# The last tile of a sparse attention kernel as 128 rows instead of 127, with the spare row dropped at the scatter

## The chip, the cores and the metric

The kernel runs on one core of one Trainium2 chip. The metric is the device time of one execution in microseconds (us), from three runs of the kernel before. The profile is of one more execution. A core has five engines that work side by side and wait for one another through semaphores: TensorE (PE, its weight loads shown as PEld), VectorE (DVE), ScalarE (ACT), GpSimd (POOL) and SyncE (SP). Transfers between the chip's main memory and the on-chip memory are done by 16 DMA engines.

## The reference, cut to what matters

```python
def reference(x, adj, Wf, bf, Wg, bg, W, bW):            # x: 3327 x 1024, adj: 3327 x 3327, 0 or 1
    h = jnp.maximum(_layernorm(x, axis=-1), 0.0)
    f = h @ Wf + bf
    g = h @ Wg + bg
    e = jax.nn.relu(f @ g.T)
    scores = jnp.where(adj > 0, e, -9e15)
    attention = jax.nn.softmax(scores, axis=1)
    return x + attention @ (h @ W + bW)
```

The graph is sparse: a node has itself and some 16 neighbours on average, so of each row of 3327 scores only a few count.

## The kernel before, in words

The rows (nodes) are handled in tiles of P = 128. There are 3327 = 25 x 128 + 127 nodes, so NT = 26 tiles, and the last one (number 25) has 127 rows; `rows(t)` gives the count.

**First part** (to about 300 us). For each tile of nodes in their given order the kernel normalises x into `hd` (main memory, one row of 1024 numbers, 4 KB, per node), reads the adjacency rows, and makes a list of up to KM = 40 neighbour numbers with the node's degree behind them, stored in `pd` (41 numbers per node). Beside that, TensorE makes A = Wf Wg^T. At its end the nodes are sorted by falling degree: `perm[p, s]` (line 594) is the number of the node that stands at place p of tile s. A place that no node is sorted to holds 0, which in this kernel is place 127 of tile 25. After the sort `make_rows()` (line 595) makes a few bias rows on PE and VectorE. Where the direct transfers of this part would have 127 rows, `pieces(t)` cuts them in two, 112 rows and 15.

**Second part** (the rest). It goes over the 26 tiles of sorted nodes. `CAPS[s]` is the largest degree that tile s may have: 37 for tile 0, then falling to 14, 13, 13, 12, 11 for tiles 21 to 25. If any node were over its cap, `bads` (line 655) would be set and a slow dense path would follow; with these inputs it does not run. For tile s:

- `prepare(s)`: GpSimd gathers the lists `pi` and the rows `hp` of the tile's own nodes by `perm` (indirect DMA, one row per partition, helper `gather`, line 621). PE transposes `hp` and multiplies it by A into `q` (lines 632, 650, 651), ScalarE copies `q` out (652).
- `dot(s, k)` for k below the cap: GpSimd gathers `G`, the rows of `hd` of everybody's k-th neighbour (line 621); VectorE multiplies it with `q` and sums along the row into one score per node (line 668, output `junk`).
- `softmax` over the scores (lines 678 to 694).
- `combine`: y = sum of score times `G`. VectorE does one step per k (line 734), ScalarE the first (732); in tiles with a cap over 13 some of the steps go through ScalarE and PE (728, 711).
- `project(s)`: GpSimd gathers the rows `xp` of x; PE transposes y (711), ScalarE copies it (744), PE multiplies with W into `ps_o` (749, 750).
- `finish(s)`: VectorE adds `ps_o` to `xp` (758), and GpSimd scatters `xp` to the output rows by `perm` (indirect DMA, line 759).

In program order `prepare(s + 2)` stands behind `project(s)`, the dots of the next chunk stand 3 ahead (`AHEAD`), and `finish(s - 1)` stands behind the dots of tile s. The framework's scheduler then sets the final order per engine. `G` has 23 buffers, so gather number i waits until gather number i - 23 has been read for the last time; `pi` has 3 buffers, `q`, `hp`, `xp` and y two. All indirect DMAs are issued by GpSimd, one after the other, and a wait at the head of its queue holds back every gather behind it.

In the last tile every one of these operations takes the partitions `[:n]` with n = 127: one gather of `pi`, one of `hp`, 11 of `G`, one of `xp` and the scatter.

Of the kernel before, what the change touches and what calls it, by code (L numbers as in the profile page):

```python
# [8 lines left out]
FP = mybir.dt.float32  # L9
I32 = mybir.dt.int32  # L10
AF = mybir.ActivationFunctionType
# [10 lines left out]
KM = 40  # L22
# [266 lines left out]
def edge_path(ctx: ExitStack, tc: tile.TileContext, x, adj, Wf, bf, Wg, bg, W, bW, out, flag):  # L289
# [23 lines left out]
    def rows(t):  # L313
        return min(P, N - t * P)
# [25 lines left out]

    perm = const.tile([P, NT], I32, name="perm")
    A_sb = wts.tile([P, KD, QW], FP, name="A_sb")
# [23 lines left out]
    with ExitStack() as part1:  # L366
# [227 lines left out]
        nc.vector.scalar_tensor_tensor(perm, ps[:, :NT], float(P), tens, op0=ALU.mult, op1=ALU.add)  # L594
        make_rows()
# [32 lines left out]
    def transposed2(to, of, n):  # L628
        for g in range(0, KD, 4):
            ps = p_t.tile([P, 4, P], FP, name="ps_t")  # L630
            for k in range(4):
                nc.tensor.transpose(ps[:, k, :n], of[:n, (g + k) * P : (g + k + 1) * P], ident[:n, :n])
            nc.scalar.copy(to[:, g : g + 4, :n], ps[:, :, :n])  # L633
# [3 lines left out]
    def prepare(s):  # L637
        n = rows(s)
        e = st[s] = {"n": n}
# [5 lines left out]
        transposed2(hT, hp, n)  # L645
        q = e["q"] = qpool.tile([P, QW], FP, name="q")
        for o in range(0, QW, QB):
            ps = p_q.tile([P, CB], FP, name="ps_q")
            for k in range(KD):
                nc.tensor.matmul(ps[:n, :QB], hT[:, k, :n], A_sb[:, k, o : o + QB], start=(k == 0), stop=False)  # L650
            nc.tensor.matmul(ps[:n, :QB], ones3[:, :n], v3[:, o : o + QB], start=False, stop=True)
            nc.scalar.copy(q[:n, o : o + QB], ps[:n, :QB])  # L652
        df = small.tile([P, 1], FP, name="df")
        nc.vector.tensor_copy(df[:n], pi[:n, KM : KM + 1])
        nc.vector.tensor_scalar(bads[:n, s : s + 1], df[:n], float(CAPS[s]), None, op0=ALU.is_gt)
        mask = e["mask"] = small.tile([P, KM], FP, name="mask")
        nc.vector.tensor_scalar(mask[:n], iotak[:n], df[:n], NEG, op0=ALU.is_ge, op1=ALU.mult)
        e["sc"] = small.tile([P, KM], FP, name="sc")
# [3 lines left out]
    def dot(s, k):  # L662
        e = st[s]
        n = e["n"]
# [3 lines left out]
        nc.vector.tensor_tensor_reduce(  # L668
            junk[:n], g[:n], e["q"][:n, :D], 1.0, e["q"][:n, D : D + 1], op0=ALU.mult, op1=ALU.add,
            accum_out=e["sc"][:n, k : k + 1],  # L670
        )

    def softmax(s, k0, k1, last):

        e = st[s]
        n = e["n"]
        sc = e["sc"][:n, k0:k1]
        nc.vector.scalar_tensor_tensor(sc, sc, 0.0, e["mask"][:n, k0:k1], op0=ALU.max, op1=ALU.add)
        nm = small.tile([P, 1], FP, name="nm")
        nc.vector.tensor_reduce(nm[:n], sc, AX.X, ALU.max, negate=True)  # L680
        if k0:
            nc.vector.tensor_tensor(nm[:n], nm[:n], e["nm"][:n], op=ALU.min)
        l = small.tile([P, 1], FP, name="l")
        nc.scalar.activation(sc, sc, AF.Exp, bias=nm[:n], accum_out=l[:n])
        if k0:
            al = small.tile([P, 1], FP, name="al")
            nc.scalar.activation(al[:n], e["nm"][:n], AF.Exp, bias=nm[:n], scale=-1.0)
            nc.vector.scalar_tensor_tensor(l[:n], e["l"][:n], al[:n], l[:n], op0=ALU.mult, op1=ALU.add)
        if last:
            rs = small.tile([P, 1], FP, name="rs")  # L690
            nc.vector.reciprocal(rs[:n], l[:n])
            if k0:
                nc.vector.tensor_tensor(al[:n], al[:n], rs[:n], op=ALU.mult)
            nc.vector.tensor_scalar(sc, sc, rs[:n], None, op0=ALU.mult)
        if k0:
            nc.scalar.activation(e["y"][:n], e["y"][:n], AF.Copy, scale=al[:n])
        e["nm"], e["l"] = nm, l
# [7 lines left out]
    def sum_transposed(e, g, first, last):  # L705

        n = e["n"]
        if first:
            e["yT"] = p_y.tile([P, KD, P], FP, name="yT_ps")
        for c in range(KD):  # L710
            nc.tensor.matmul(  # L711
                e["yT"][:, c, :n], g[:n, c * P : (c + 1) * P], ident[:n, :n], is_transpose=True,
                start=(first and c % 4 == 0), stop=(last and c % 4 == 3), skip_group_check=True,
            )

    def combine(s, k0, k1, last):
        e = st[s]
        n = e["n"]
        if not k0:
            e["y"] = ypool.tile([P, D], FP, name="y")  # L720
        y = e["y"][:n]
        e["first"] = True
        pe = on_tensor(s, k0, k1) if last else []
        for k in range(k0, k1):
            p = e["sc"][:n, k : k + 1]
            g = G[s, k]
            if k in pe:
                nc.scalar.activation(g[:n], g[:n], AF.Copy, scale=p)  # L728
                sum_transposed(e, g, e["first"], False)
                e["first"] = False  # L730
            elif k == 0:
                nc.scalar.activation(y, g[:n], AF.Copy, scale=p)  # L732
            else:
                nc.vector.scalar_tensor_tensor(y, g[:n], p, y, op0=ALU.mult, op1=ALU.add)  # L734

    def project(s):
        e = st[s]
        n = e["n"]
        e["xp"] = xpool.tile([P, D], FP, name="xp")
        gather(e["xp"][:n], x[:, :], perm[:n, s : s + 1])  # L740
        yT = yTpool.tile([P, KD, P], FP, name="yT")
        sum_transposed(e, e["y"], e["first"], True)
        for g in range(0, KD, 4):
            nc.scalar.copy(yT[:, g : g + 4, :n], e["yT"][:, g : g + 4, :n])  # L744
        e["o"] = []
        for o in range(OH):
            ps = p_o.tile([P, CB], FP, name="ps_o")
            for k in range(KD):
                nc.tensor.matmul(ps[:n], yT[:, k, :n], W_sb[:, k, o * CB : (o + 1) * CB], start=(k == 0), stop=False)  # L749
            nc.tensor.matmul(ps[:n], ones3[:, :n], bW3[:, o * CB : (o + 1) * CB], start=False, stop=True)  # L750
            e["o"].append(ps)

    def finish(s):
        e = st[s]
        n = e["n"]
        for o in range(OH):
            xo = e["xp"][:n, o * CB : (o + 1) * CB]
            nc.vector.tensor_add(xo, e["o"][o][:n], xo)  # L758
# [91 lines left out]
```

## Time and profile before

| | us |
|---|---|
| median of the three runs (lowest, highest) | 1500.97 (1500.28, 1507.38) |
| profiled execution, its own time | 1504.68 |
| span of the profiled execution, first to last instruction | 1502.9 |
| VectorE busy | 1274.7 (85%) |
| PE busy | 1165.0 (78%) |
| GpSimd busy | 891.9 (59%) |
| ScalarE busy | 442.9 (29%) |

A row of the groups gives the line, engine and operation, output <- input by the program's names, then "xcount | busy us, mean ns of one | idle time of the engine just before them, and what ended it". In the rows in order of time the first number is the start in us from the span's start, the second the length in us; in square brackets stands the idle time of that engine before it and what ended it. In the answers on DMA the digits are tenths of the 16 engines' time in 40 equal slices of the window that was asked for, and under them stand the GB/s that were moved in each slice; "us to landing" runs from the issue of a transfer to its last byte.

### The profile page before, as it was taken

Reading aid. Unit: us, or ns where it says so; the run is one execution under the profiler, and the core shown is the slowest. Engines: PE = TensorE matmul, PEld = TensorE weight load, DVE = VectorE, ACT = ScalarE, POOL = GpSimd, SP = SyncE. Lnnn points to the kernel's source line nnn. Section 1 sums busy time; section 2 is a strip of 40 time slices with the busy share of each in tenths; the row PEclk is TensorE's granted clock in tenths of the full one; section 3 lists DMA queues with packets and bytes.
Section 4 is the critical chain, followed back from the end, with each engine's and each line's share of the span. In section 5 each row is a group of like instructions: output and inputs, shape, how many; then the busy total and the mean of one; then the engine's idle time right before and its main releaser. Section 6 shows DMA issues by size and latency. Waiting matters only on the chain.

```text
span 1502.9 us, 13875 instructions
## 1 busy us (share of the span) xinstructions
PE 1165.0 (78%) x4242; PEld 660.4 (44%) x4242; DVE 1274.7 (85%) x2645; ACT 442.9 (29%) x673; POOL 891.9 (59%) x627
## 2 busy tenths in 40 slices
PE   1259899284298989999898889999999899695262
PEld 1125453052165545555554455555554455342030
DVE  5878887959979999999888899999999999696360
ACT  6656676111144223342222212223121211110000
POOL 7677767346567667646655565667576666374310
PEclk9999899687698999999998989999999999897676
DMA  9797887268687898868766777788787777384310
GB/s 339 286 357 272 321 282 259 82 233 324 205 308 277 292 323 309 297 225 322 265 206 233 263 281 281 280 293 282 252 276 257 253 255 232 126 321 101 86 44 16
DMA packets 124445, 372.57 MB, mean 248 GB/s; under 512 B 41025, under 2 KB 41425, under 8 KB 121033
## 3 DMA queue, kind: packets, MB, share of 16 engines
q0 software_dynamic: 106288, 286.92, 55.6%
q1 hardware_dynamic: 10860, 70.49, 12.9%
q10 hardware_dynamic: 7212, 14.18, 2.5%
q8 instruction: 35, 0.57, 0.2%
q14 instruction: 50, 0.41, 0.1%
HBM read 343.63 MB, written 27.80 MB: 247 GB/s over the span
## 4 chain that ended last, share of the span: by engine, by line
DVE 28%; PE 24%; issue 20%; POOL 12%; DMA 11%; ACT 3%; POOLq 0%; ACTq 0%; DVEq 0%
DVE y L734 12%; PE ps_o L749 12%; DMA G<-hd,pi 9%; DVE junk L668 6%; POOL r L446 5%; POOL G L621 5%; PE ps_q L650 5%; PE yT_ps L711 4%; DVE cand L455 3%; PE ps_A L522 2%; DMA pi<-pd,perm 1%; PE ps_A L540 1%; DVE xp L758 1%; ACT r L445 1%; DVE sc L668 1%
## 5 line engine op out<-in xcount | busy, mean ns | idle before, releaser
L621 POOL DMA_INDIRECT G<-hd,pi x468 | 572.6, 1223 | 307.2 <-ACT y L732 95.5
L668 DVE CUSTOM_DVE_ANT_0 junk<-G,q 128x1024 bf16<-128x1024 f32 (+1 forms) x468 | 601.1, 1284 | 80.7 <-DMA G<-hd,pi 78.1
L650 PE MATMUL ps_q<-A_sb,hT 128*128 128x342 f32 (+1 forms) x1248 | 395.1, 466 | 74.8 <-ACT q L652 64.8
L734 DVE SCALAR_TENSOR_TENSOR y<-G,sc,y 128x1024 f32<-128x1024 f32 (+1 forms) x320 | 411.3, 1285 | 4.8 <-ACT y L732 2.8
L749 PE MATMUL ps_o<-W_sb,yT 128*128 128x512 f32 (+1 forms) x832 | 388.0, 621 | 9.9 <-ACT yT L744 9.7
L650 PEld LDWEIGHTS ps_q<-A_sb,hT 128*128 128x128 f32 (+1 forms) x1248 | 232.8, 194 | 195.4 <-ACT q L652 67.1
L749 PEld LDWEIGHTS ps_o<-W_sb,yT 128*128 128x128 f32 (+1 forms) x832 | 161.2, 199 | 208.7 <-issue 190.0
L446 POOL TENSOR_TENSOR r<-r,iotaj 128x3327 f32<-128x3327 f32 (+1 forms) x26 | 187.8, 7227 | 74.6 <-ACT r L445 59.8
L455 DVE MAX8 cand<-r 128x8 f32<-128x208 f32 (+2 forms) x416 | 134.3, 362 | 34.8 <-POOL r L446 34.8
L652 ACT COPY q<-ps_q 128x342 f32<-128x342 f32 (+1 forms) x78 | 32.7, 449 | 342.3 <-DVE sc L668 249.2
L728 ACT ACTIVATE G<-G,sc 128x1024 f32<-128x1024 f32 x122 | 129.0, 1137 | 0.0
L522 PE MATMUL ps_A<-WgT,WfT 128*128 128x512 f32 x256 | 122.4, 638 | 2.9 <-ACT WfT L496 2.9
L711 PE MATMUL yT_ps<-ident,G 128*128 128x128 f32 x976 | 116.8, 277 | 2.1 <-ACT G L728 2.1
L711 PEld LDWEIGHTS yT_ps<-ident,G 128*128 128x128 f32 x976 | 108.5, 142 | 12.6 <-ACT G L728 5.5
L633 ACT COPY hT<-ps_t 128x512 f32<-128x512 f32 (+1 forms) x52 | 30.1, 593 | 192.2 <-PE ps_q L650 159.9
L711 PE MATMUL yT_ps<-ident,y 128*128 128x128 f32 (+1 forms) x208 | 34.4, 320 | 67.4 <-DVE y L734 49.8
L744 ACT COPY yT<-yT_ps 128x512 f32<-128x512 f32 (+1 forms) x52 | 27.8, 586 | 198.2 <-PE yT_ps L711 198.0
L522 PEld LDWEIGHTS ps_A<-WgT,WfT 128*128 128x128 f32 x256 | 51.4, 205 | 75.9 <-issue 66.0
L759 POOL DMA_INDIRECT out_dram<-xp,perm x26 | 35.0, 1346 | 77.6 <-DVE xp L758 71.8
L445 ACT ACTIVATE r<-a 128x3327 f32<-128x3327 int32 (+1 forms) x26 | 77.1, 2967 | 8.7 <-issue 4.8
L758 DVE TENSOR_TENSOR xp<-ps_o,xp 128x512 f32<-128x512 f32 (+1 forms) x52 | 35.7, 686 | 34.5 <-PE ps_o L750 34.4
L711 PEld LDWEIGHTS yT_ps<-ident,y 128*128 128x128 f32 (+1 forms) x208 | 28.7, 166 | 72.5 <-DVE y L734 37.3
(134 smaller groups left out, 760.0 us busy)
## 6 DMA issues: line engine op xcount, KB each, us to landing
a<-in_adj_dram SPq DMA_DIRECT2D x25, 1663.5 KB, 9.0
xt<-in_x_dram SPq DMA_DIRECT2D x25, 512.0 KB, 4.9
hd<-xt ACTq DMA_DIRECT2D x25, 512.0 KB, 5.4
G<-hd,pi POOLq DMA_INDIRECT x468, 6.3
wr<-in_L_gnn_Wg_dram SPq DMA_DIRECT2D x8, 512.0 KB, 6.5
wr<-in_L_gnn_Wf_dram SPq DMA_DIRECT2D x8, 512.0 KB, 5.7
W_sb<-in_L_gnn_W_dram SPq DMA_DIRECT2D x1, 4096.0 KB, 16.5
a<-in_adj_dram SPq DMA_DIRECT2D x1, 1455.6 KB, 11.1
```

Of the source, the lines that this page charges most:

```text
L445: nc.scalar.activation(r[:n], a[:n], AF.Relu, accum_out=deg[:n, t : t + 1])
L446: nc.gpsimd.tensor_mul(r[:n], r[:n], iotaj[:n])
L455: nc.vector.max(cand[:n, s * 8 : s * 8 + 8], r[:n, s * SW : min(N, (s + 1) * SW)])
L522: nc.tensor.matmul(ps, WfT[:, k, :], WgT[:, k, o * CB : (o + 1) * CB], start=(k == 0), stop=(k == KD - 1))
L621: nc.gpsimd.indirect_dma_start(out=to, out_offset=None, in_=table, in_offset=bass.IndirectOffsetOnAxis(ap=idx, axis=0),)
L650: nc.tensor.matmul(ps[:n, :QB], hT[:, k, :n], A_sb[:, k, o : o + QB], start=(k == 0), stop=False)
L668: nc.vector.tensor_tensor_reduce(junk[:n], g[:n], e["q"][:n, :D], 1.0, e["q"][:n, D : D + 1], op0=ALU.mult, op1=ALU.add, accum_out=e["sc"] ...
L711: nc.tensor.matmul(e["yT"][:, c, :n], g[:n, c * P : (c + 1) * P], ident[:n, :n], is_transpose=True, start=(first and c % 4 == 0), stop=(la ...
L728: nc.scalar.activation(g[:n], g[:n], AF.Copy, scale=p)
L734: nc.vector.scalar_tensor_tensor(y, g[:n], p, y, op0=ALU.mult, op1=ALU.add)
L749: nc.tensor.matmul(ps[:n], yT[:, k, :n], W_sb[:, k, o * CB : (o + 1) * CB], start=(k == 0), stop=False)
L758: nc.vector.tensor_add(xo, e["o"][o][:n], xo)
```

## The change

The second part takes all 26 tiles as 128 rows. All slices `[:n]` go, so the last tile's 15 indirect DMAs and its arithmetic have 128 partitions. Partition 127 of the last tile has `perm` = 0, so it gathers the list, the rows and the neighbours of node 0 a second time. To keep its result away from the output, a new column `final` holds the last column of `perm` with N = 3327 added where the partition number is at least 127; the last tile's scatter goes by `final`, with a bounds check of N - 1 that is no error, so that this row is skipped. `bads` is still taken over the first `rows(s)` partitions alone. The first part has two VectorE instructions of one column more. The other scatters go by `perm` without a check, as before.

```diff
+    final = const.tile([P, 1], I32, name="final")
...
         nc.vector.scalar_tensor_tensor(perm, ps[:, :NT], float(P), tens, op0=ALU.mult, op1=ALU.add)
+        over = c1.tile([P, 1], FP, name="over")
+        nc.vector.tensor_scalar(over, part, float(rows(NT - 1)), float(N), op0=ALU.is_ge, op1=ALU.mult)
+        nc.vector.tensor_tensor(final, perm[:, NT - 1 : NT], over, op=ALU.add)
         make_rows()
...
-        gather(pi[:n], pd[:, :], perm[:n, s : s + 1])
+        gather(pi, pd[:, :], perm[:, s : s + 1])
...
-        gather(hp[:n], hd[:, :], perm[:n, s : s + 1])
+        gather(hp, hd[:, :], perm[:, s : s + 1])
...
-        nc.vector.tensor_scalar(bads[:n, s : s + 1], df[:n], float(CAPS[s]), None, op0=ALU.is_gt)
+        nc.vector.tensor_scalar(bads[: rows(s), s : s + 1], df[: rows(s)], float(CAPS[s]), None, op0=ALU.is_gt)
...
-        gather(g[:n], hd[:, :], e["pi"][:n, k : k + 1])
+        gather(g, hd[:, :], e["pi"][:, k : k + 1])
...
-        gather(e["xp"][:n], x[:, :], perm[:n, s : s + 1])
+        gather(e["xp"], x[:, :], perm[:, s : s + 1])
...
         ins = nc.gpsimd.indirect_dma_start(
             out=out[:, :],
-            out_offset=bass.IndirectOffsetOnAxis(ap=perm[:n, s : s + 1], axis=0),
-            in_=e["xp"][:n],
+            out_offset=bass.IndirectOffsetOnAxis(ap=perm[:, s : s + 1] if s < N // P else final, axis=0),
+            in_=e["xp"],
             in_offset=None,
+            bounds_check=None if s < N // P else N - 1,
+            oob_is_err=s < N // P,
         )
```

The order in which the instructions stand is the same before and after on every engine, but for the two added ones on VectorE: `over` far ahead in the first part, `final` right behind `perm`. This is the end of GpSimd's queue before the change (line, operation, output <- input, shape, count); the gathers of `hp` and `pi` for the last tile stand 22 and 16 gathers of `G` ahead of it:

```order
L621 DMA G<-hd,pi 128x1024
L621 DMA xp<-in_x_dram,perm 128x1024
L621 DMA G<-hd,pi 128x1024 x7
L621 DMA G<-hd,pi 127x1024 x5
L759 DMA out_dram<-xp,perm 3327x1024
L621 DMA G<-hd,pi 127x1024
L621 DMA xp<-in_x_dram,perm 128x1024
L621 DMA G<-hd,pi 127x1024 x5
L759 DMA out_dram<-xp,perm 3327x1024
L621 DMA xp<-in_x_dram,perm 127x1024
L759 DMA out_dram<-xp,perm 3327x1024 x2
```

And the end of the same queue in the changed kernel, where line 627 is the gather and 758 the scatter:

```order
L627 DMA G<-hd,pi 128x1024
L627 DMA xp<-in_x_dram,perm 128x1024
L627 DMA G<-hd,pi 128x1024 x12
L758 DMA out_dram<-xp,perm 3327x1024
L627 DMA G<-hd,pi 128x1024
L627 DMA xp<-in_x_dram,perm 128x1024
L627 DMA G<-hd,pi 128x1024 x5
L758 DMA out_dram<-xp,perm 3327x1024
L627 DMA xp<-in_x_dram,perm 128x1024
L758 DMA out_dram<-xp,perm 3327x1024
L758 DMA out_dram<-xp,final 3327x1024
```

Nothing has moved: the 127 has become 128 (the x12 are the seven gathers of tile 24 and the five of tile 25), and the last scatter goes by `final`.

More of the change, by code (lines that the diff above doesn't have):

```diff
@@ L626, in gather, with transposed2 @@
         )
-    def transposed2(to, of, n):
+    def transposed2(to, of):
         for g in range(0, KD, 4):
@@ L631, in transposed2 @@
             for k in range(4):
-                nc.tensor.transpose(ps[:, k, :n], of[:n, (g + k) * P : (g + k + 1) * P], ident[:n, :n])
-            nc.scalar.copy(to[:, g : g + 4, :n], ps[:, :, :n])
+                nc.tensor.transpose(ps[:, k, :], of[:, (g + k) * P : (g + k + 1) * P], ident)
+            nc.scalar.copy(to[:, g : g + 4, :], ps)
     st = {}
     def prepare(s):
-        n = rows(s)
-        e = st[s] = {"n": n}
+        e = st[s] = {}
         pi = e["pi"] = psp.tile([P, PW], I32, name="pi")
-        gather(pi[:n], pd[:, :], perm[:n, s : s + 1])
+        gather(pi, pd[:, :], perm[:, s : s + 1])
         hp = hpool.tile([P, D], FP, name="hp")
-        gather(hp[:n], hd[:, :], perm[:n, s : s + 1])
+        gather(hp, hd[:, :], perm[:, s : s + 1])
         hT = hTpool.tile([P, KD, P], FP, name="hT")
-        transposed2(hT, hp, n)
+        transposed2(hT, hp)
         q = e["q"] = qpool.tile([P, QW], FP, name="q")
@@ L711, in sum_transposed @@
             nc.tensor.matmul(
-                e["yT"][:, c, :n], g[:n, c * P : (c + 1) * P], ident[:n, :n], is_transpose=True,
+                e["yT"][:, c, :], g[:, c * P : (c + 1) * P], ident, is_transpose=True,
                 start=(first and c % 4 == 0), stop=(last and c % 4 == 3), skip_group_check=True,
```

62 lines of the change are left out of this document (28 added, 34 removed).

## The prediction

> **What bounds the kernel now.** I read the page first, for the engines' shares and the course of the traffic over the span.
>
> ```profile
> span 1502.9 us, 13875 instructions
> PE 1165.0 (78%) x4242; PEld 660.4 (44%) x4242; DVE 1274.7 (85%) x2645; ACT 442.9 (29%) x673; POOL 891.9 (59%) x627
> DVE  5878887959979999999888899999999999696360
> GB/s 339 286 357 272 321 282 259 82 233 324 205 308 277 292 323 309 297 225 322 265 206 233 263 281 281 280 293 282 252 276 257 253 255 232 126 321 101 86 44 16
> ```
>
> VectorE bounds the second part: nines from slice 13 to 33, one slice being 37.6 us. Only the last six slices fall off: first a dip (slice 34), then the last tile, where the traffic drops to 16 GB/s. The change touches nothing else, so I looked at the windows from 1255 us on. Second view: the groups with shapes kept apart, and VectorE's waits from 1262 to 1440 us.
>
> ```profile
> L668 DVE CUSTOM_DVE_ANT_0 junk<-G,q 128x1024 bf16<-128x1024 f32 x457 | 587.0, 1285 | 44.6 <-DMA G<-hd,pi 42.0
> L668 DVE CUSTOM_DVE_ANT_0 junk<-G,q 127x1024 bf16<-127x1024 f32 x11 | 14.1, 1281 | 36.0 <-DMA G<-hd,pi 36.0
> DVE junk L668 <- DMA G<-hd,pi: 50.0, 9, 22.2
> ```
>
> The 11 dots of the last tile wait 36.0 us for their gathers, nearly as much as the other 457 together; with the two waits just before, VectorE stands still for 50.0 us here. Third view: the DMA answers for two windows, each around one scatter with nothing beside it: tile 24's, 128 rows, and tile 25's, 127 rows.
>
> ```profile
> DMA  0000000000089899898921100000001000000000
> GB/s 28 28 0 28 28 28 28 28 28 28 28 339 367 367 424 424 367 395 367 452 85 57 56 28 28 0 0 0 0 0 56 0 0 0 0 0 0 0 0 0
> out_dram<-xp,perm POOLq DMA_INDIRECT x1, 4.1
> ...
> DMA  0000016611000000000000000000000000000000
> GB/s 0 0 11 11 0 1 44 22 23 23 17 6 23 23 28 23 28 28 23 28 28 23 28 28 23 28 28 23 28 28 23 28 28 23 28 28 0 0 0 0
> DMA packets 2053, 0.57 MB, mean 20 GB/s; under 512 B 1921, under 2 KB 1921, under 8 KB 2048
> out_dram<-xp,perm POOLq DMA_INDIRECT x1, 25.7
> ```
>
> The first moves its half megabyte at 339 to 452 GB/s with eight or nine tenths of the 16 engines busy and lands in 4.1 us. The second has a share that rounds to zero tenths and 23 to 28 GB/s, a sixteenth of 424, and lands in 25.7. So a transfer of 127 rows goes through one DMA engine; the rest do only very small packets (1921 of the 2053). GpSimd's rows in order of time show that such a transfer costs more to issue, too, and what it does to its neighbours:
>
> ```profile
> 1266.80 2.87 POOL L621 DMA_INDIRECT hp<-hd,perm  x1 [0.30 <-issue]
> 1277.52 0.93 POOL L621 DMA_INDIRECT G<-hd,pi  x1 [0.30 <-issue]
> 1301.92 2.63 POOL L621 DMA_INDIRECT pi<-pd,perm  x1 [23.47 <-DMA G<-hd,pi]
> 1296.03 1.28 DVE L668 CUSTOM_DVE_ANT_0 junk<-G,q 128x1024 bf16<-128x1024 f32 x1 [13.05 <-DMA G<-hd,pi]
> 1310.44 1.28 DVE L668 CUSTOM_DVE_ANT_0 junk<-G,q 128x1024 bf16<-128x1024 f32 x1 [0.89 <-DMA G<-hd,pi]
> 1419.20 1.28 DVE L668 CUSTOM_DVE_ANT_0 junk<-G,q 127x1024 bf16<-127x1024 f32 x1 [22.23 <-DMA G<-hd,pi]
> ```
>
> The last tile's `hp` is issued at 1266.80. The gathers of 128 rows behind it have a sixteenth of their rows on its engine and land when it has passed: VectorE waits 13.05 us until 1296.03, and GpSimd 23.47 us before it can load `pi` over an old buffer.
>
> **The change part by part.** Everything below is against the profiled execution's own 1504.68 us (span 1502.9), which is 3.7 above the median of the runs, 1500.97; I take the sum off that median at the end.
>
> *A, the stall at 1283 to 1311 us.* With `hp` at 128 rows it lands like any other gather:
>
> ```profile
> DMA to landing us min/median/max: 2.7/6.0/8.3
> DMA to landing us min/median/max: 4.4/25.3/27.6
> ```
>
> (the gathers' landing at 1100 to 1260 us, and at 1340 to 1440, where the last tile's are.) The gather whose dot waits until 1296.03 was issued at 1269.98 and would land by 1278; VectorE is free for it at 1282.98. Both waits go, 13.05 + 0.89 = 13.9 us. What is late next is PE:
>
> ```profile
> 1255.00:1296.00 41.00, 40.02 (x137) 21.83 (x136) 27.98 (x42) 5.76 (x11) 17.75 (x14) 1.00 0.60 196
> 1307.52 2.65 PE L650 MATMUL ps_q<-A_sb,hT 128*128 128x342 f32 x4 [12.01 <-ACT q L652]
> 1262.57 1.32 PE L650 MATMUL ps_q<-A_sb,hT 128*128 128x342 f32 x4
> ```
>
> PE is busy 40.02 of the 41 us (first pair behind the length), idles only 12.01, and then starts slowly: four matmuls in 2.65 us instead of 1.32. Without the pause it gains 12.0 + 1.3 = 13.3. VectorE's additions at L758 wait for PE soon after, so A is worth 13.3, between 11 and 14.
>
> *B, the dots of the last tile.* The 36.0 us of waits go if the gathers keep up. They do by the order: the first five stand ahead of tile 22's scatter, the other six behind it, and the `xp` gather among them waits for that scatter's landing. Before:
>
> ```profile
> 1339.20 1.03 POOL L621 DMA_INDIRECT xp<-in_x_dram,perm  x1 [3.75 <-DMA out_dram<-xp,perm]
> 1391.04 0.98 POOL L621 DMA_INDIRECT xp<-in_x_dram,perm  x1 [19.60 <-DMA out_dram<-xp,perm]
> 1363.05 3.47 POOL L621 DMA_INDIRECT G<-hd,pi  x1 [0.30 <-DVE sc L668]
> ```
>
> The 19.60 becomes the 3.75 of a tile earlier, and each of the 11 issues 0.93 + 0.30 instead of 2.5 to 3.5 + 0.30. GpSimd is then through its last gather about when VectorE begins the last tile's dots, save the very last, whose buffer is freed by tile 23's last step of y. Two things are left in B. First, PE restarts slowly on tile 23's y:
>
> ```profile
> 1378.27 1.28 DVE L734 SCALAR_TENSOR_TENSOR y<-G,sc,y 128x1024 f32<-128x1024 f32 x1
> 1379.69 1.94 PE L711 MATMUL yT_ps<-ident,y 128*128 128x128 f32 x8 [17.70 <-DVE nm L680]
> 1391.39 0.38 PE L750 MATMUL ps_o<-bW,ones 3*128 3x512 bf16 x1
> 1398.77 0.38 PE L750 MATMUL ps_o<-bW,ones 3*128 3x512 bf16 x1
> 1364.03 1.28 DVE L668 CUSTOM_DVE_ANT_0 junk<-G,q 128x1024 bf16<-128x1024 f32 x1
> 1365.23 1.28 DVE L734 SCALAR_TENSOR_TENSOR y<-G,sc,y 128x1024 f32<-128x1024 f32 x1
> ```
>
> From y's end (1379.47) to the first half of `ps_o` (1391.77) are 12.3 us. VectorE has nine large steps of 1.20 us (the distance of the last two starts) and three small ones of about 0.1 before it adds that half, 11.1, so it will wait 1.2 here. Second, one step at the end was stretched while GpSimd wrote a 127-row transfer:
>
> ```profile
> L694 DVE TENSOR_SCALAR sc<-sc,rs 127x11 f32<-127x11 f32 x1 | 1.2, 1162 | 0.0
> L694 DVE TENSOR_SCALAR sc<-sc,rs 128x11 f32<-128x11 f32 x2 | 0.5, 227 | 0.0
> ```
>
> That gives 0.9 back. B = 36.0 - 1.2 + 0.9 = 35.7, between 31 (some 5 us of other waits come up behind) and 37.
>
> *C, the last scatter.* It ends the kernel: 25.7 us to landing against 4.1 for the same shape of 128 rows, also alone. It stands last in GpSimd's queue, and nothing hides it. The bounds check and the skipped row show nowhere in this trace; I take 4.3, nearest to the lone 128-row scatter, and as ends 4.1 and 6.3, the median of all 26. C = 25.7 - 4.3 = 21.4, between 19.4 and 21.6; the check could also put rows on fewer engines, which is a rival.
>
> *D, PE at the end.* Behind the last dot stand two projections one after the other, which the change leaves alone:
>
> ```profile
> 1440.53 9.02 PE ps_o L749 x16
> 1449.87 7.06 PE ps_o L749 x16
> 1342.47 1.03 PE L711 MATMUL yT_ps<-ident,y 128*128 128x128 f32 x8
> ```
>
> The first half ran 1.96 us longer than the second, after PE had stood still since 1399. Now its pause is about 8.6 us: from the end of y of tile 23 VectorE needs 21 steps of 1.20 plus 3.1 of small ones and the wait, 28.3, and PE is done 19.7 after it. The nearest row is the slow start after 12.01 us above, so I take no gain, and 2.9 as the end (1.96, and 0.9 on the transposes, 1.94 at 1379.69 against 1.03). [...]
>
> *Edits at nothing.* The arithmetic on 128 instead of 127 partitions costs the same (1285 and 1281 ns above). `over` sits in the first part beside other work. `final` sits on the path between `perm` and `make_rows()`; a small operation of this kind is 0.17 us long at most:
>
> ```profile
> 278.28 0.17 DVE L597 TENSOR_TENSOR ne<-deg,cnt 128x26 f32<-128x26 f32 x1
> ```
>
> Sum: 13.3 + 35.7 + 21.4 - 0.2 = 70.2 us. 1504.68 - 70.2 = 1434.5 for an execution like the profiled one; 1500.97 - 70.2 = 1430.8 against the median, and I give 1431. All low ends (11 + 31 + 19.4 - 0.2 = 61.2) give 1440, all high ones (14 + 37 + 21.6 + 2.9 = 75.5) 1425.
>
> **The rivals.**
>
> *The scatter stays on few engines.* The check may make GpSimd treat the rows one by one, so that they all go to one engine again. Nothing in the profile has such a check, for or against. C is lost, A and B stay: 1501 - 48.8 = 1452.
>
> *GpSimd becomes late.* If `xp` goes on waiting 19.60 us for the scatter ahead of it, the five gathers behind it stay late and VectorE keeps the wait of 22.23 at 1419.20: gain 48.0, time 1453. The 3.75 one tile earlier speaks against it.
>
> *The rows are spread already, and nothing changes.* Then the last tile's transfers would be slow for what they read, not for their count, and the time stays at 1501. [...]
>
> *Slower: the check is made row by row.* If GpSimd must compare each of 128 indices and issue each row by itself at the price of a short issue, 0.93 us, the last scatter takes 119 us instead of 25.7. Loss 93.4, against 48.8 gained: 1501 + 44.6 = 1546. It decides from 0.58 us a row (25.7 + 48.8 = 74.5, over 128). Against it: all 128 rows of a gather are issued in 0.93 us, 7 ns a row, and a comparison should not cost eighty times that.
>
> **How the numbers follow.** The forecast has 0.82; the scatter on few engines 0.06, GpSimd late 0.05, no change 0.04, slower 0.03. The forecast's own range is 1425 to 1440; with the two partial cases at 1452 and 1453, and a few us at the low end for what runs differ by, the range is 1422 to 1453. Faster by over 0.5% (7.5 us, about what a measurement here can tell from no change): 0.82 + 0.06 + 0.05 = 0.93; same 0.04; slower 0.03.
>
> **What would show it.** In the profile after: the landing of the gathers from 1340 us on near 6 us, not 25.3; no wait of `junk` for `G` over 2 us from 1262 us on; the `pi` load of the last tile waiting a few us instead of 23.47; PE without the pause of 12.01; the last scatter landing within 7 us, at over 300 GB/s; small packets gone. Wrong would be: one engine's 25 GB/s in any transfer of the last tile, a wait of VectorE for PE above some 5 us in its place, or a last scatter that GpSimd takes long to issue.

## The result and the profile after

The changed kernel takes 1438.18 us (median of 4 runs, 1436.85 to 1438.43) against 1503.68 us of the kernel before (4 runs beside them, 1500.28 to 1507.38). The ratio is 0.9562, 95% interval 0.9533 to 0.9591: 65.5 us less. The profiled execution after took 1437.97 us with a span of 1436.2; before it was 1504.68 and 1502.9. By the two spans the gain is 66.7 us, and the comparison below splits these 66.7.

First the page of the changed kernel: the span, the busy time of the engines, VectorE's course over the span and the traffic.

```profile
span 1436.2 us, 13878 instructions
PE 1160.7 (81%) x4242; PEld 657.3 (46%) x4242; DVE 1266.7 (88%) x2647; ACT 442.7 (31%) x673; POOL 873.6 (61%) x627
DVE  3878888977979999998988889999999988999991
GB/s 340 292 348 294 325 302 260 86 140 402 236 224 310 310 315 276 302 314 206 279 324 210 230 261 281 292 286 271 266 287 258 257 254 228 252 275 256 263 30 32
```

The busy times are those of before within 2.1%; what went is idle time. VectorE's nines now reach the last slice but one, and from slice 25 to slice 38 the traffic stays at 228 GB/s or more. The group of the dots and VectorE's waits from 1262 to 1437 us:

```profile
L672 DVE CUSTOM_DVE_ANT_0 junk<-G,q 128x1024 bf16<-128x1024 f32 x468 | 600.7, 1284 | 31.5 <-DMA G<-hd,pi 28.8
DVE xp L757 <- PE ps_o L750: 20.6, 4, 8.5
DVE y L735 <- ACT y L733: 1.9, 3, 1.2
```

One form of the dots is left, and their wait over the whole run is 28.8 us where it was 42.0 and 36.0. In this window no wait for a DMA is left at all (50.0 us before); what remains is VectorE waiting for the projections. (The longest of these, 8.5 us and 6.7, stand at the end and are as long in the kernel before, 8.55 and 6.73; they are not new.) The gathers from 1340 us on land as the prediction said, in some 6 us and no longer in 25.3:

```profile
DMA to landing us min/median/max: 4.2/5.8/6.2
```

GpSimd's rows in order of time show why. The first is the last tile's `hp`, the second its `pi`, the third the `xp` that waited 19.60 us:

```profile
1265.17 1.25 POOL L627 DMA_INDIRECT hp<-hd,perm  x1 [0.30 <-issue]
1279.79 0.95 POOL L627 DMA_INDIRECT pi<-pd,perm  x1 [3.97 <-DMA G<-hd,pi]
1351.10 1.87 POOL L627 DMA_INDIRECT xp<-in_x_dram,perm  x1 [2.83 <-DMA out_dram<-xp,perm]
```

The issue of `hp` fell from 2.87 to 1.25 us, the wait ahead of `pi` from 23.47 to 3.97, that ahead of `xp` to 2.83. PE's rows for the same places:

```profile
1293.33 0.77 PE L638 MATMUL ps_t<-ident,hp 128*128 128x128 f32 x5
1293.93 1.32 PE L655 MATMUL ps_q<-A_sb,hT 128*128 128x342 f32 x4
1295.08 1.04 PE L713 MATMUL yT_ps<-ident,y 128*128 128x128 f32 x8
1297.11 7.03 PE L749 MATMUL ps_o<-W_sb,yT 128*128 128x512 f32 x16
1387.05 1.94 PE L713 MATMUL yT_ps<-ident,y 128*128 128x128 f32 x8 [8.85 <-DVE sc L697]
1389.72 8.64 PE L749 MATMUL ps_o<-W_sb,yT 128*128 128x512 f32 x16 [0.73 <-ACT yT L744]
```

The four matmuls behind the last tile's transposes follow at once, in 1.32 us; before they came after a pause of 12.01 us and took 2.65. The pause ahead of tile 24's transposes is 8.85 us now.

To split the gain I set the same instruction of both kernels side by side. These are the rows of the kernel before, then those of the changed one: PE at the q of the last tile but one, tile 24's softmax, tile 24's transposes, the last scatter.

```profile
1289.70 4.87 PE L650 MATMUL ps_q<-A_sb,hT 128*128 128x342 f32 x16
1371.29 0.16 DVE L678 SCALAR_TENSOR_TENSOR sc<-sc,mask 128x12 f32<-128x12 f32 x1
1437.86 1.94 PE L711 MATMUL yT_ps<-ident,y 128*128 128x128 f32 x8 [15.32 <-DVE y L734]
1474.94 2.56 POOL L759 DMA_INDIRECT out_dram<-xp,perm  x1 [15.66 <-DVE xp L758]
```

```profile
1288.29 1.99 PE L655 MATMUL ps_q<-A_sb,hT 128*128 128x342 f32 x6
1355.70 0.16 DVE L681 SCALAR_TENSOR_TENSOR sc<-sc,mask 128x12 f32<-128x12 f32 x1
1423.65 1.00 POOL L758 DMA_INDIRECT out_dram<-xp,final  x1 [15.61 <-DVE xp L757]
```

| stretch | before | after | gain | the prediction's term |
|---|---|---|---|---|
| to PE at 1289.70 / 1288.29 | | | 1.4 | none: one execution against another |
| to tile 24's softmax | 81.59 | 67.41 | 14.2 | A, 13.3 |
| to tile 24's transposes | 66.57 | 31.35 | 35.2 | B, 35.7 |
| to the last scatter's issue | 37.08 | 36.60 | 0.5 | D, 0 |
| to the end of the span | 27.96 | 12.55 | 15.4 | C, 21.4 |

Three terms are right within a microsecond; C is 6.0 short. The first row is a difference between two executions that no term covers, so differences of about that size in the other rows mean little. The last scatter in the changed kernel (the DMA answer from 1422 us to the end of the span, 0.36 us a slice) did what was forecast, and more:

```profile
DMA  0000000009997000000000000000000000000000
GB/s 0 0 0 0 0 0 23 0 23 369 427 381 289 23 23 0 0 0 0 0 0 23 0 0 0 0 0 0 0 0 0 0 0 0 0 0 0 0 0 0
...
q14 instruction: 5, 0.04, 1.0%
...
out_dram<-xp,final POOLq DMA_INDIRECT x1, 3.5
```

It lands in 3.5 us (25.7 before) at up to 427 GB/s. But the span ends 9.05 us behind its landing, where it ended 2.3 behind it before. The instructions of GpSimd's own queue in that time, before and then after (their count, the shortest, median and longest in ns, and the first and last start):

```profile
L821 POOLq INC_SWDGE_SEM  x1: 400/400/400, 1500.8 to 1500.8; - x1
...
L846 POOLq DRAIN  x3: 46/103/885, 1501.2 to 1502.7; - x3
```

```profile
L822 POOLq COMPARE_BRANCH  x1: 62/62/62, 1424.0 to 1424.0; - x1
L822 POOLq EVENT_SEMAPHORE  x5: 17/43/43, 1426.7 to 1429.3; - x5
L822 POOLq INC_SWDGE_SEM  x1: 1320/1320/1320, 1429.4 to 1429.4; - x1
...
L847 POOLq DRAIN  x3: 46/103/4642, 1430.8 to 1436.0; - x3
```

After its last issue GpSimd jumps over the dense path (COMPARE_BRANCH); five packets on the instruction queue q14 fall into that time. Only at 1429.4 comes INC_SWDGE_SEM, then a DRAIN, and with it the end. Two things have changed: the jump, which lay under the slow scatter, now ends 2.2 us later than the scatter's landing; and INC_SWDGE_SEM and DRAIN have grown from 0.400 and 0.885 us to 1.320 and 4.642.

### The profile page after: what moved, and what is told of

It is laid out like the page before. It is cut to its first block, busy times and chain, and to the rows that moved or that the text cites. A ratio compares the mean times of both kernels' runs of the same rounds, so it can differ in the third digit from the quotient of the medians.

```text
span 1436.2 us, 13878 instructions
## 1 busy us (share of the span) xinstructions
PE 1160.7 (81%) x4242; PEld 657.3 (46%) x4242; DVE 1266.7 (88%) x2647; ACT 442.7 (31%) x673; POOL 873.6 (61%) x627
## 4 chain that ended last, share of the span: by engine, by line
PE 35%; DVE 27%; issue 18%; POOL 10%; DMA 6%; ACT 3%; POOLq 0%; ACTq 0%; SPq 0%; DVEq 0%
PE ps_o L749 16%; DVE y L735 12%; PE ps_q L655 10%; POOL r L449 6%; DVE junk L672 5%; PE yT_ps L713 5%; DMA G<-hd,pi 4%; POOL G L627 4%; DVE cand L458 3%; PE ps_A L525 2%; ACT r L448 1%; PE ps_A L543 1%; DVE xp L757 1%; DVE sc L672 1%; DVE lst L465 1%
## 5 line engine op out<-in xcount | busy, mean ns | idle before, releaser
L672 DVE CUSTOM_DVE_ANT_0 junk<-G,q 128x1024 bf16<-128x1024 f32 x468 | 600.7, 1284 | 31.5 <-DMA G<-hd,pi 28.8
L655 PE MATMUL ps_q<-A_sb,hT 128*128 128x342 f32 x1248 | 394.5, 466 | 63.5 <-ACT q L657 53.5
L735 DVE SCALAR_TENSOR_TENSOR y<-G,sc,y 128x1024 f32<-128x1024 f32 x320 | 411.3, 1285 | 4.7 <-ACT y L733 2.9
L749 PE MATMUL ps_o<-W_sb,yT 128*128 128x512 f32 x832 | 387.1, 620 | 9.8 <-ACT yT L744 9.5
L655 PEld LDWEIGHTS ps_q<-A_sb,hT 128*128 128x128 f32 x1248 | 233.2, 194 | 183.4 <-ACT q L657 55.6
L749 PEld LDWEIGHTS ps_o<-W_sb,yT 128*128 128x128 f32 x832 | 161.0, 198 | 207.9 <-issue 189.1
L657 ACT COPY q<-ps_q 128x342 f32<-128x342 f32 x78 | 32.8, 449 | 328.7 <-DVE sc L672 225.2
L639 ACT COPY hT<-ps_t 128x512 f32<-128x512 f32 x52 | 30.1, 593 | 192.1 <-PE ps_q L655 159.8
L713 PE MATMUL yT_ps<-ident,y 128*128 128x128 f32 x208 | 33.8, 316 | 56.6 <-DVE y L735 35.7
L757 DVE TENSOR_TENSOR xp<-ps_o,xp 128x512 f32<-128x512 f32 x52 | 35.6, 685 | 34.2 <-PE ps_o L750 34.0
## 6 DMA issues: line engine op xcount, KB each, us to landing
W_sb<-in_L_gnn_W_dram SPq DMA_DIRECT2D x1, 4096.0 KB, 14.2
```

Of the source, the lines that this page charges most:

```text
L655: nc.tensor.matmul(ps[:, :QB], hT[:, k, :], A_sb[:, k, o : o + QB], start=(k == 0), stop=False)
L672: nc.vector.tensor_tensor_reduce(junk, g, e["q"][:, :D], 1.0, e["q"][:, D : D + 1], op0=ALU.mult, op1=ALU.add, accum_out=e["sc"][:, k : k ...
L713: nc.tensor.matmul(e["yT"][:, c, :], g[:, c * P : (c + 1) * P], ident, is_transpose=True, start=(first and c % 4 == 0), stop=(last and c % ...
L735: nc.vector.scalar_tensor_tensor(y, g, p, y, op0=ALU.mult, op1=ALU.add)
L749: nc.tensor.matmul(ps, yT[:, k, :], W_sb[:, k, o * CB : (o + 1) * CB], start=(k == 0), stop=False)
L757: nc.vector.tensor_add(xo, e["o"][o], xo)
```

## The experiments

They ran in three sets, each on a chip of its own with the kernel before beside it: 1567.29 us (e1 to e4, 9 runs, 1561.29 to 1572.05), 1504.24 (e5 to e8, 11 runs, 1498.46 to 1509.02), 1505.68 (e9 to e11, 9 runs, 1500.57 to 1508.07). Times are compared within a set only; between sets, only ratios to the kernel before are. In e1 to e4 my theory was that C is short because the jump and the closing steps, hidden before, have become bare. The rival was the bounds check.

### e1: `hp` alone

```diff
-        gather(hp[:n], hd[:, :], perm[:n, s : s + 1])
+        gather(hp, hd[:, :], perm[:, s : s + 1])
```

> The kernel before with one edit: the last tile's gather of hp takes 128 rows, everything else of that tile stays at 127. By the theory that one transfer of 127 rows on one DMA engine holds up the gathers behind it, stall A goes alone: the wait of 13.05 us of VectorE for G and GpSimd's wait of 23.47 us before the pi load shrink to a few us, PE's pause of 12.01 us goes, and the time falls by about 14 us (13.3 in the prediction; 14.2 read off the changed kernel's trace), while the 36.0 us of waits of the last tile's dots and the 25.7 us of the last scatter stay. Rival: the stall comes from the load of pi or from buffers being reused, not from hp; then the waits stay and the time changes by less than 2 us.

Measured: 1552.08 us (1547.31 to 1556.89), ratio 0.991, interval 0.9879 to 0.994: 15.2 us less, or 9 to 19 by the interval, around the 14.2 of A. The dots of the last tile in this kernel:

```profile
L668 DVE CUSTOM_DVE_ANT_0 junk<-G,q 127x1024 bf16<-127x1024 f32 x11 | 14.1, 1282 | 36.6 <-DMA G<-hd,pi 36.6
```

Their wait stays whole (36.0 before). GpSimd's waits ahead of `pi` in the whole run (total, times, longest):

```profile
POOL pi L621 <- DMA G<-hd,pi: 7.8, 3, 4.4
```

The longest is 4.4 us where it was 23.47, and PE has no pause over 0.5 us in the 40 us behind the issue of the last tile's `hp` (12.01 before). So A belongs to the one gather of `hp`, and A and B are separate.

### e2: the last scatter alone

The kernel before with `final`, the gather of the last `xp` and the last scatter as in the change (two of the 15 transfers at 128 rows).

```diff
-            out_offset=bass.IndirectOffsetOnAxis(ap=perm[:n, s : s + 1], axis=0),
-            in_=e["xp"][:n],
+            out_offset=bass.IndirectOffsetOnAxis(ap=perm[:, s : s + 1] if s < N // P else final, axis=0),
+            in_=e["xp"],
...
+            bounds_check=None if s < N // P else N - 1,
+            oob_is_err=s < N // P,
```

> The kernel before with only the last scatter changed: xp is gathered and scattered as 128 rows, with the spare row dropped by the bounds check; pi, hp, G and the arithmetic stay at 127. The prediction's term C says 21.4 us less. The changed kernel's trace says otherwise: its scatter lands 3.5 us after issue instead of 25.7, but the span ends 12.55 us after issue instead of 27.96. By the theory that some closing work of about 9 us behind the landing, before hidden by the slow scatter, is now bare, this kernel gains 15.4 us; by the prediction's sum 21.4.

Measured: 1539.63 us (1537.8 to 1545.16), ratio 0.9825, interval 0.9787 to 0.9864: 27.7 us less, between 21 and 33, over both expectations. The times of this set scatter too much to choose; the trace does it:

```profile
L827 POOLq INC_SWDGE_SEM  x1: 460/460/460, 1540.9 to 1540.9; - x1
...
L852 POOLq DRAIN  x3: 46/103/1130, 1541.4 to 1543.1; - x3
```

The span ends 8.1 us after the scatter's issue (12.55 in the changed kernel, 27.96 before), so the scatter alone is worth 19.9 us of the end here. The closing steps are short, though the scatter is as fast as in the changed kernel and has the bounds check. That is the first sign that my theory lacks something.

### e3: no bounds check

The changed kernel with its last scatter sent to a spare buffer of 3328 rows, without a check and with no row to skip; the last 127 rows of the output are left out.

```diff
+    spare = dram.tile([N + 1, D], FP, name="spare")
...
-            out=out[:, :],
+            out=out[:, :] if s < N // P else spare[:, :],
...
-            bounds_check=None if s < N // P else N - 1,
-            oob_is_err=s < N // P,
```

> The changed kernel with the last scatter of 128 rows going to a spare buffer of 3328 rows in main memory, with no bounds check and no row dropped; so the last 127 rows of the output are left out. Theory that the closing work belongs to GpSimd's queue whatever the scatter's kind: the span still ends about 12.5 us after the scatter's issue and the time stays within 1 us of the changed kernel. Rival, that the bounds check or the dropped row lengthens GpSimd's last steps (its drain is 4.64 us in the changed kernel and 0.89 before): the drain falls to about 0.9 and the end comes about 4 to 5 us sooner, 8 us after the issue.

Measured: one run, 1500.19 us. Its closing steps:

```profile
L821 POOLq INC_SWDGE_SEM  x1: 1320/1320/1320, 1491.6 to 1491.6; - x1
...
L846 POOLq DRAIN  x3: 46/103/4642, 1492.9 to 1498.1; - x3
```

To the nanosecond those of the changed kernel, and the span ends 12.4 us after the issue (12.55 in the changed kernel). The check and the skipped row cost nothing that the end shows: this rival is out.

### e4: no dense path, no jump

```diff
-        with tc.If(bad > 0):
-            dense_path(tc, x, adj, Wf, bf, Wg, bg, W, bW, out)
```

> The changed kernel without the dense path and the branch over it; the dense path does not run with these inputs, so the output is the same. Theory that part of the closing work is the jump over the dense path: in the changed kernel GpSimd branches 0.35 us behind the scatter's issue, and its next steps come 2.7 and 5.0 us after the branch. Without the jump the span should end 3 to 5 us sooner after the scatter's issue (7.5 to 9.5 us instead of 12.55) and the time fall by as much. Rival, that it is GpSimd's own clearing up after its last transfer: the end stays at 12 to 12.5 us behind the issue and the time within 1 us.

Measured: 1488.18 us (1486.53 to 1497.43), ratio 0.9518, interval 0.9469 to 0.9567. The span ends 6.5 us after the scatter's issue instead of 12.55, which is more than the 3 to 5 us that I expected to go. (By the run times it is 12.0 us under the one run of e3, but its own runs lie 11 us apart.) There is no INC_SWDGE_SEM, but a long DRAIN is still there, beside the scatter's transfer instead of behind it:

```profile
L845 POOLq DRAIN  x3: 46/109/5929, 1479.1 to 1485.6; - x3
```

So the jump and what GpSimd does behind it hold 6 us of the changed kernel's end. This does not say why the closing steps took 4.7 us less before the change; e6 asks that.

### e5: the changed kernel again

> The changed kernel itself, so that the other kernels of this set have it on their own chip. If the gain of the profiled pair (66.7 us of 1502.9) is what the change is worth, the ratio is 0.956 here as well, 65 to 70 us. If the sum of its parts as measured on the noisier chip is right (15.2 for hp alone, 27.7 for the scatter alone, and what the other gathers bring, 35.2 by the traces), it is 78 us, a ratio near 0.950.

Measured: 1437.03 us (6 runs, 1434.35 to 1445.89), ratio 0.9562, interval 0.9536 to 0.9588, the first result once more: 67.2 us less. The sum of 78 us from the parts does not come back. Of the 27.7 us of e2, 19.9 stand at the end of its trace, which is below the interval of its times; where the rest comes from stays open, and I go by the traces there.

### e6: the gathers without the scatter

The changed kernel with the last scatter as before the change.

```diff
-            out_offset=bass.IndirectOffsetOnAxis(ap=perm[:, s : s + 1] if s < N // P else final, axis=0),
-            in_=e["xp"],
+            out_offset=bass.IndirectOffsetOnAxis(ap=perm[: rows(s), s : s + 1], axis=0),
+            in_=e["xp"][: rows(s)],
...
-            bounds_check=None if s < N // P else N - 1,
-            oob_is_err=s < N // P,
```

> The changed kernel with the old last scatter: all gathers of 128 rows, but the result of the last tile written as 127 rows. Theory: the gathers' part (14.2 + 35.2 + 0.4) is independent of the scatter, so this kernel stands 50 us below the one before and 15 to 16 us above the changed one; its span ends 28 us after the last scatter's issue, the scatter itself lands in some 25.7 us, and the closing steps INC_SWDGE_SEM and DRAIN take 0.4 and 0.9 us again. Rival (the scatter's part is worth the 21.4 us of the prediction and the gathers less): 44 to 46 us below the one before and 21 us above the changed one.

Measured: 1457.76 us (1456.28 to 1462.27), ratio 0.9699, interval 0.9674 to 0.9724: 46.5 us under the kernel before and 20.7 above e5. That is close to the rival's forecast of 44 to 46 and 21. The row of its last scatter, the landing and the closing steps:

```profile
1422.97 2.58 POOL L758 DMA_INDIRECT out_dram<-xp,perm  x1 [15.63 <-DVE xp L757]
```

```profile
out_dram<-xp,perm POOLq DMA_INDIRECT x1, 25.6
```

```profile
L820 POOLq INC_SWDGE_SEM  x1: 1320/1320/1320, 1448.8 to 1448.8; - x1
...
L845 POOLq DRAIN  x3: 46/103/4642, 1450.1 to 1455.3; - x3
```

The scatter is the slow one of before, with 25.6 us to landing, and yet the closing steps are those of the changed kernel: the span ends 32.6 us after the issue, not 28. So my theory falls in its larger half. INC_SWDGE_SEM and DRAIN have not become bare; they stand behind the landing in both kernels, and have grown by 0.92 + 3.76 = 4.7 us **through the edits outside the scatter**, whatever the scatter does. These are the 14 gathers and the arithmetic on 128 partitions; that the gathers have a part is shown by e10 and e11, in which only gathers differ, but no run shows that the whole 4.7 is theirs. The scatter's part is 32.6 - 12.55 = 20.1 us by the traces, 20.7 by the medians. By the same count the rest of the change brings 14.2 + 35.2 + 0.5 - 4.7 = 45.2, against 46.5 measured.

### e7: a scatter of 120 rows

```diff
+        m = P if s < N // P else 120
...
-            out_offset=bass.IndirectOffsetOnAxis(ap=perm[:n, s : s + 1], axis=0),
-            in_=e["xp"][:n],
+            out_offset=bass.IndirectOffsetOnAxis(ap=perm[: min(n, m), s : s + 1], axis=0),
+            in_=e["xp"][: min(n, m)],
```

> The kernel before with only its last scatter cut from 127 to 120 rows; 7 rows of the output are left unwritten. [...] Theory B (every count but a multiple of 16 goes through one engine): 25.7 x 120 / 127 = 24.3 us, and the run is 1.4 us shorter. [...]

Measured, with 7 rows of the output left out: one run, 1482.41 us, 21.8 less than before. The DMA answer from 1470 us to the end (0.27 us a slice) and the closing steps:

```profile
GB/s 0 0 0 0 0 0 0 0 0 0 0 0 0 31 0 31 93 232 216 124 185 201 371 371 62 62 0 0 0 0 0 0 0 31 0 0 0 0 0 0
DMA packets 149, 0.53 MB, mean 50 GB/s; under 512 B 24, under 2 KB 24, under 8 KB 144
...
out_dram<-xp,perm POOLq DMA_INDIRECT x1, 4.4
```

```profile
L822 POOLq INC_SWDGE_SEM  x1: 400/400/400, 1478.5 to 1478.5; - x1
...
L847 POOLq DRAIN  x3: 46/103/885, 1479.0 to 1480.4; - x3
```

Theory B, with its 24.3 us, falls: 120 rows land in 4.4 us at up to 371 GB/s, though 120 is no multiple of 16, and only 24 packets are very small (1921 with 127 rows). So a tile that isn't full need not be slow. The runs have three counts: 127 rows land in 25.7 us, 120 in 4.4 and 128, with nothing beside them, in 3.5 to 4.1. What in the count decides is not shown, and no view shows the engines one by one.

### e8 and e9: the jump ahead of the last scatter

Both move the last scatter behind the branch, so that GpSimd jumps while PE still works on the last projection; `flast` is `final` plus N times the flag, which is meant to skip the whole scatter if the dense path has run; in no run here did it. The diff shows e9.

```diff
-        e["xp"] = xpool.tile([P, D], FP, name="xp")
+        e["xp"] = xlast if s % 2 else xpool.tile([P, D], FP, name="xp")
...
+        nc.vector.scalar_tensor_tensor(flast, ps[:, 0:1], float(N), final, op0=ALU.mult, op1=ALU.add)
...
         with tc.If(bad > 0):
             dense_path(tc, x, adj, Wf, bf, Wg, bg, W, bW, out)
+        nc.gpsimd.indirect_dma_start(
+            out=out[:, :],
+            out_offset=bass.IndirectOffsetOnAxis(ap=flast, axis=0),
+            in_=xlast,
+            in_offset=None,
+            bounds_check=x.shape[0] - 1,
+            oob_is_err=False,
+        )
```

> The changed kernel with its last scatter moved behind the jump over the dense path: GpSimd jumps, fetches code and does INC_SWDGE_SEM while the last projection still runs on TensorE, then waits for the last sum and issues the scatter. If the dense path had run, an index past the bounds skips the scatter, so nothing is left out. Theory (the closing steps on GpSimd's queue, bare since the scatter became short, hold the 6 us that the prediction missed): the span ends 6.5 us after the scatter's issue as in the kernel without the dense path, and the kernel is 5 to 6.5 us faster than the changed one. Rival (a DRAIN of 4.6 us comes behind any last scatter whatever stands before it): the span ends 10 us or more after the issue, and the gain is 2.5 us or less.

Measured: 1428.5 us (1425.78 to 1431.05), ratio 0.95, but this run answers nothing: by a slip of mine `xlast` was the buffer of the tiles with even numbers, so that tile 24 was scattered a second time, the last tile's rows were left out, and the scatter waited for nothing. In e9 it is the buffer of the odd tiles, to which tile 25 belongs.

> The kernel with the jump ahead of the last scatter once more, now with the last tile in the buffer that is scattered (in e8 it was the tile before, so that the scatter did not wait for the last sum). Theory: the jump, INC_SWDGE_SEM and what the long DRAIN stands for are done some 9 us before the last sum, so the span ends 6.5 to 8 us after the scatter's issue instead of 12.55, and the kernel is 4.6 to 6 us faster than the changed one, ratio to the one before 0.952 to 0.953. Rival, from e8's trace: there the DRAIN ended 6.95 us after the scatter's issue, later than INC_SWDGE_SEM's own 6 us would make it; if 4.6 us come behind the landing (3.5 us) of any last scatter, the end is 9 us or more after the issue and the gain under 3.5 us.

Measured: 1433.61 us (5 runs, 1431.97 to 1436.37), ratio 0.9523, interval 0.9503 to 0.9543. GpSimd's row of the last scatter and its closing steps:

```profile
1428.08 1.00 POOL L827 DMA_INDIRECT out_dram<-xlast,flast  x1 [15.61 <-DVE xlast L759]
```

```profile
L825 POOLq INC_SWDGE_SEM  x1: 1300/1300/1300, 1416.9 to 1416.9; - x1
...
L858 POOLq DRAIN  x3: 46/109/5940, 1427.8 to 1434.4; - x3
```

INC_SWDGE_SEM is done 10 us ahead of the scatter, and the span (1434.6) ends 6.5 us after the issue, as the theory had it: 6.0 us of the changed kernel's end are gone by the traces. (The profiled execution itself is the slowest of the five: level with the changed kernel's at 1001 us, it was 4 us behind at 1067.) Set against e5's ratio, 0.9523 / 0.9562 = 0.996, about 6 us; with both intervals put together 0.9925 to 0.9993. It clearly beats the kernel before; the changed one it beats by little, in a comparison over two chips that only just excludes no gain. The long DRAIN begins ahead of the scatter's issue here and ends some 4.7 us after GpSimd has written the transfer: it now lies beside the landing, but still ends last.

### e10 and e11: what makes the closing steps long

The kernel before with some gathers of the last tile at 128 rows: in e11 `pi`, `hp` and `xp`, in e10 also every second `G`. Arithmetic and scatter stay at 127.

```diff
-        gather(pi[:n], pd[:, :], perm[:n, s : s + 1])
+        gather(pi, pd[:, :], perm[:, s : s + 1])
-        gather(hp[:n], hd[:, :], perm[:n, s : s + 1])
+        gather(hp, hd[:, :], perm[:, s : s + 1])
-        gather(e["xp"][:n], x[:, :], perm[:n, s : s + 1])
+        gather(e["xp"], x[:, :], perm[:, s : s + 1])
...
-        gather(g[:n], hd[:, :], e["pi"][:n, k : k + 1])
+        m = n if k % 2 else P
+        gather(g[:m], hd[:, :], e["pi"][:m, k : k + 1])
```

> The kernel before with pi, hp, xp and every second gather of G of the last tile (6 of 11) as 128 rows, the arithmetic and the scatter as 127. It asks how the closing steps grow with the number of gathers that are changed: INC_SWDGE_SEM and DRAIN took 0.40 and 0.885 us with none or one of the last tile's 15 transfers changed, 0.46 and 1.13 with two, 1.32 and 4.642 with 14 and with 15. Theory (they grow with the number): with these 9 about 0.9 and 2.8. Rival (two levels, by something else that the last gathers decide): one of the known pairs exactly. The stall of the dots: 11 waits of 36.0 us in all stand against none; the five gathers that stay at 127 rows still land 25 us after their issue, so I expect 10 to 25 us to stay, and the run 20 to 40 us under the one before.

> The kernel before with only pi, hp and xp of the last tile gathered as 128 rows; all 11 gathers of G, the arithmetic and the scatter stay at 127. Closing steps by the theory of e10 (they grow with the number of transfers changed, 3 here): about 0.5 and 1.4; by its rival one of the known pairs exactly. Stalls: A (14.2 by the traces) goes, the dots' 36 us stay; 1488 to 1492 us where the one before takes 1504.

Measured, one run each: e10 1485.49 us (20.2 less than before), e11 1490.86 (14.8 less). The dots of the last tile, e10 and then e11, and the closing steps of all kernels:

```profile
L669 DVE CUSTOM_DVE_ANT_0 junk<-G,q 127x1024 bf16<-127x1024 f32 x11 | 14.1, 1281 | 30.4 <-DMA G<-hd,pi 30.4
L668 DVE CUSTOM_DVE_ANT_0 junk<-G,q 127x1024 bf16<-127x1024 f32 x11 | 14.1, 1281 | 37.6 <-DMA G<-hd,pi 37.6
```

| kernel | transfers at 128 rows, of 15 | INC_SWDGE_SEM, us | DRAIN, us |
|---|---|---|---|
| before; e7 (scatter of 120) | 0 | 0.400 | 0.885 |
| e1 | 1 | 0.400 | 0.885 |
| e2 | 2 | 0.460 | 1.130 |
| e11 | 3 | 0.360 | 0.722 |
| e10 | 9 | 0.460 | 1.130 |
| e6 | 14 | 1.320 | 4.642 |
| changed; e3; e5 | 15 | 1.320 | 4.642 |

(e9, with 15, has 1.300; its DRAIN lies over the scatter and can't be compared.)

For the closing steps neither expectation holds. They don't grow with the number of changed transfers (3 give less than none, 9 as much as 2), and though e10 shows a known pair, that of e2, the pair of e11 is new. The two move together: from each row to the next, DRAIN changes by 4.08 times what INC_SWDGE_SEM does. What they count stays open. The stalls of e11 came as expected: A is gone, the dots' wait is whole, and 1490.86 lies in the 1488 to 1492. Of that wait, e10 shows that six of the eleven gathers buy only a fifth: the five that stay at 127 rows leave 30.4 of the 37.6 us, above the 10 to 25 that I expected.

## Why the prediction came out as it did

The direction, the mechanism and three of the four terms were right. The forecast of 1431 was 7.2 us under the 1438.18: 2.7 because the median of the kernel before rose from 1500.97 to 1503.68 with its fourth run, 4.7 because 65.5 us went instead of 70.2 (the 0.2 between is rounding). That the sum comes as close is in part luck: by the traces C alone was 6.0 too high, and 2.8 of that came back from A, D and the 1.4 us that no term covers.

*A, 14.2 for 13.3.* The pause of 12.01 and the slow start went as said. e1 puts A on `hp` (15.2 us), and e11, with `pi` and `xp` besides, gains no more (14.8).

*B, 35.2 for 35.7.* All waits for gathers went, and the new wait for `ps_o` is the one that was forecast:

```profile
1370.74 0.69 DVE L757 TENSOR_TENSOR xp<-ps_o,xp 128x512 f32<-128x512 f32 x1 [1.21 <-PE ps_o L750]
1386.82 0.23 DVE L697 TENSOR_SCALAR sc<-sc,rs 128x11 f32<-128x11 f32 x1
```

1.21 for 1.2. The step at L697 (694 before) is back at 0.23 as well. Whether the 0.9 credited for it came on top can't be told: 35.2 lies between 36.0 - 1.2 = 34.8 without it and 35.7 with it, and no run isolates it.

*D, 0.5 for 0.* The pause of 8.85 us (8.6 forecast) left PE slow: 1.94 us for the eight transposes and 8.64 for the first half, at granted clocks of 0.50 and 0.82, against 1.04 and 7.03 at 1295.08 and 1297.11, both at 1.00. Most of the 0.5 is the first half, which took 9.02 before. That the slow start after 12.01 us is the nearest row was a misreading. In the trace of the kernel before, outside the window that the prediction looked at, stand these transposes:

```profile
704.55 1.09 PE L711 MATMUL yT_ps<-ident,y 128*128 128x128 f32 x8 [2.54 <-DVE y L734]
844.11 1.97 PE L711 MATMUL yT_ps<-ident,y 128*128 128x128 f32 x8 [3.45 <-DVE y L734]
```

The second eight ran at a granted clock of 0.50, the first at 1.00. So the choice of no gain could have been read off, and the 2.9 us at the high end left out.

*C, 15.4 for 21.4: the step that failed.* "C = 25.7 - 4.3 = 21.4" takes the end to stand as far behind the landing after as before. The landing was even better, 3.5 us. But the step looked at the transfer and not at what its engine does behind it: it put the jump and the growth of the closing steps at nothing, without a reason. INC_SWDGE_SEM started 25.9 us after the issue before (1500.8 - 1474.94) and 5.75 after the change (1429.4 - 1423.65): 20.1 gained, 1.3 under the term, since it now starts 5.4 us behind COMPARE_BRANCH (1424.0), 2.2 us later than the landing. From there to the end it takes 4.7 us more, and that is a price of the other edits (e6), not of the scatter. 20.1 - 4.7 = 15.4. Of the jump, 2.7 us pass from COMPARE_BRANCH (1424.0) to the next step (1426.7); what fills them is not shown. e9 shows that the jump can be moved under other work, for 6.0 us of the end.

*The rivals.* The scatter on few engines: out, 427 GB/s. GpSimd late: out, `xp` waits 2.83 us and no dot waits. Rows spread already: out, by the result and by e7. The check made row by row: out, the issue takes 1.00 us and e3 has the same end without a check.

What remains unsettled: what INC_SWDGE_SEM and the DRAIN behind it count, and with it which of the edits outside the scatter lengthened them.

## What to carry to other kernels

Where an indirect transfer of 127 rows is as slow as here (25.7 us against 3.5 with 128), pad it to 128, and do so for all of a chain: six of eleven gathers brought a fifth of the waits. (A count of 120 is fast too, 4.4 us, but the seven rows left over would need a second transfer, which no run here has.) When a slow transfer at the end of a kernel becomes fast, read what its issuing engine still has to do behind it, step by step, because the end can move to that (it came 9.05 us behind the landing here, 2.3 before); a branch over unused code can go ahead of the last transfer, under work that runs anyway (e9). And when a term comes out short, test the parts crosswise (the one without the other, both ways), since a cost that shows at one part's place may be the other part's.

## What the runs showed of the hardware that was not expected

- INC_SWDGE_SEM and the DRAIN at the end of GpSimd's queue took 0.360 and 0.722, 0.400 and 0.885, 0.460 and 1.130, or 1.320 and 4.642 us in kernels that differ in the row counts of the last tile's transfers; the last three pairs came back to the nanosecond in several kernels.
- A scatter of 120 rows with nothing beside it lands in 4.4 us, one of 127 in 25.6 or 25.7, one of 128 in 3.5 to 4.1.
- A jump over unused code took GpSimd 5.4 us from COMPARE_BRANCH at 1424.0 to INC_SWDGE_SEM at 1429.4.
- The kernel before took 1567.29 us on one chip where it took 1504.24 and 1505.68 on two others.
